# Unused matrix products placed ahead of the first stage of a convolution-attention kernel

## The chip, the cores and the metric

The kernel runs on one core of a Trainium2 chip. The metric is the device time of one execution in microseconds (us); lower is better. A core has five engines that run side by side, each working through its own instructions in order: TensorE (PE in the profile; its weight loads are listed as PEld), VectorE (DVE), ScalarE (ACT), GpSimd (POOL) and SyncE (SP), the last of which only issues transfers here.

## The reference, cut to what matters

The input `x` holds four images of 384 channels and 48 by 48 pixels. One attention layer with eight heads of 48 channels is computed, and its query gets a convolution added to it:

```python
local = conv_general_dilated(x, conv_w, (1, 1), 'SAME', feature_group_count=C)   # 7x7, depthwise
local = local * inv + (bn_beta - bn_mean * inv)
x_norm = layernorm(x_flat) * ln_gamma + ln_beta        # over the 384 channels of a token
q, k, v = x_norm @ qkv_w.T + qkv_b                     # split into 8 heads of 48
q = q + layernorm(local_flat)
out = softmax(q @ k.T * 48 ** -0.5) @ v                # 2304 tokens per image
out = x_flat + out @ proj_w.T + proj_b
```

## The kernel before, in words

Channels lie on the 128 partitions in three chunks. The four images are worked through in turn, each in five row tiles of 8 or 10 image rows (384 or 480 tokens). For one row tile the attention goes in twelve slots. In each slot TensorE multiplies queries and keys in products over 64 partitions (L1143; queries and keys are held as a rounded part and a rest, in the type that the program calls HALF, `float32r`, so three products make one score), ScalarE takes the exponential (L1151), and TensorE multiplies with the values in plain fp32 (L1158). In the profile a plain fp32 product appears as two matmul records with a weight load each, a `float32r` product as one.

VectorE computes the depthwise convolution of the next row tile in between, one tap at a time (L367). A list of time budgets, worked out when the program is built, sets how many taps are issued at which point of the TensorE program; so the order on every engine is fixed by the program text.

Ahead of the row tiles comes a first stage, for the keys, values and queries of image 0. Its order is written out by hand:

- SP loads the first image rows (`slab`), the weights (`staged`) and the rest of image 0 (`xn`) through one queue (L116). ACT's queue loads the small vectors.
- DVE builds `packing`, a set of 0/1 matrices that reorder channels (L222, L224), and `natural`, the taps with the batch norm folded in (L228 to L233).
- TensorE runs `warm(WARM)`, 14 products of two constant matrices whose result nobody reads (L1201). Then `pack()` multiplies `packing` by `natural` (L242), from which ACT copies `vec` (L249): the taps, shifts and gains that later steps use.
- `bias_rows()` makes two small tables on DVE (L276 to L280).
- The first 384 tokens are normalised in three blocks: means of `slab` (L729), centring on DVE (L644), squares on ACT (L583), means of those (L729), the root on ACT (L652 to L654) and on DVE (L666, L667), the scaling (L724). Meanwhile ACT scales the weights by the gains (L943, L950, L951).
- Then TensorE makes values, queries and keys group by group (L729 again, through `project`), and DVE's first convolution taps (L363, L367) and the later groups' norms run beside it.

PSUM tiles come from one pool of four double banks (`two_banks`), taken in turn. The SBUF tiles that matter here come from rotating buffers with a tag: `sq` has two, `acc` three.

The lines around the change are these:

```python
    def warm(n):
        m = two_banks()[:, 0, 0:P]
        for _ in range(n):
            nc.tensor.matmul(m, lhsT=mean_w, rhs=ident, start=True, stop=True)

    warm(WARM)
    pack()
    bias_rows()
```

Of the kernel before, what the change touches and what calls it, by code (L numbers as in the profile page):

```python
# [10 lines left out]
F32 = mybir.dt.float32  # L11
HALF = mybir.dt.float32r
# [4 lines left out]
P = 128  # L17
# [33 lines left out]
def unshifted_pass(  # L51
# [16 lines left out]
    nc = tc.nc  # L68
# [14 lines left out]
    GM = max(ROWS) * W  # L83
# [5 lines left out]
    def size(a):  # L89
        return a.stop - a.start  # L90
# [6 lines left out]
    work = ctx.enter_context(tc.tile_pool(name="work", bufs=2))  # L97
# [10 lines left out]
    def two_banks(name="r"):  # L108
        return ps.tile([P, 2, 512], F32, tag="r", name=name)
# [102 lines left out]
    for c in range(CC):  # L212
        for r, n, first in ((0, HD, 0), (64, HD, 1), (48, 16, 6), (112, 16, 7)):
            head = first + 2 * c if first < 6 else first
            ch = head * HD + (16 * c if first >= 6 else 0)
            while n:
                part = min(n, P - ch % P)
                pieces.append((c, r, ch // P, ch % P, part))
                r, n, ch = r + part, n - part, ch + part
# [17 lines left out]
    def pack():  # L237
        m = two_banks()[:, 0, 0 : CC * (T0 + 3)].rearrange("p (c v) -> p c v", c=CC)
        for c in range(CC):
            mine = [pair for pair in pairs if pair[0] == c]  # L240
            for pair in mine:
                nc.tensor.matmul(  # L242
                    m[:, c, :],
                    lhsT=packing[:, pairs.index(pair), :],
                    rhs=natural[:, pair[1], :],
                    start=pair == mine[0],
                    stop=pair == mine[-1],
                )
        nc.scalar.copy(vec, m)  # L249
# [23 lines left out]
    def bias_rows():  # L273

        rows = chosen_rows.rearrange("p a (j x) -> p a j x", j=2)
        nc.vector.memset(chosen_rows, 0.0)  # L276
        nc.vector.tensor_copy(
            rows[:, 0, :, 0:HD], ident[:, 0 : 2 * HD].rearrange("p (j d) -> p j d", j=2)
        )
        nc.vector.tensor_copy(  # L280
            rows[:, 1:4, :, HD:64],
            ident[:, 0 : 2 * HD].rearrange("p (j c r) -> p c j r", j=2, c=CC),
        )
# [610 lines left out]
    rows = {}  # L894
# [303 lines left out]
    def warm(n):  # L1198
        m = two_banks()[:, 0, 0:P]
        for _ in range(n):  # L1200
            nc.tensor.matmul(m, lhsT=mean_w, rhs=ident, start=True, stop=True)  # L1201

    warm(WARM)
    pack()
    bias_rows()

# [304 lines left out]
    for i, at in enumerate(pieces_out):  # L1511
        ao, n = aos[i], size(at)
        if i == 3:
            judge[1](two_banks()[:, 0, :])
        r, r2 = two_banks(), two_banks()
# [17 lines left out]
def conv_attention(tc: tile.TileContext, *args):  # L1533
    nc = tc.nc
    few = NH * max(ROWS) * 48 // P
    with tc.tile_pool(name="keep", bufs=1) as keep:
        inside = keep.tile([P, few], F32, tag="inside", name="inside")
        outside = keep.tile([P, few], F32, tag="outside", name="outside")
        ones = keep.tile([P, 1], F32, tag="ones_col", name="ones_col")
        total = keep.tile([1, 1], F32, tag="total", name="total")  # L1540
        flag = keep.tile([1, 1], mybir.dt.int32, tag="flag", name="flag")
        counts = []
        nc.vector.memset(inside, 1.0)
        nc.vector.memset(ones, 1.0)

        def compare():
            nc.vector.tensor_scalar(outside, inside, 0.5, None, ALU.is_lt)

        def count(m):
            counts.append(m[0:1, :few])  # L1550
            nc.tensor.matmul(counts[0], lhsT=ones, rhs=outside, start=True, stop=True)

        def decide():
            nc.vector.tensor_reduce(total, counts[0], AX.X, ALU.add)
            nc.vector.tensor_copy(flag, total)

        def read():
            return nc.values_load(flag[0:1, 0:1])

        n_outside = unshifted_pass(tc, *args, inside, (compare, count, decide, read))  # L1560
        with tc.If(n_outside > 0):
            shifted_pass(tc, *args)
# [505 lines left out]
```

## Time and profile before

| What | Value |
|---|---|
| Median of 3 runs | 2723.55 us (2722.94 to 2723.92) |
| Profiled execution | span 2720.3 us from its first to its last instruction; no time of its own is listed beside that, and the median of the runs lies 3.25 us above the span |
| TensorE busy | 2707.9 us, 100% of the span |
| VectorE busy | 2314.8 us, 85% |
| ScalarE busy | 1671.1 us, 61% |
| GpSimd busy | 592.7 us, 22% |
| Granted TensorE clock | 9 (90% or more) in each of the 40 slices of the page |

A row of a timeline gives the start and the length in us, the engine, the line and the operation, the tile written and the tile read, and the count of merged records; a bracket tells how long the engine stood idle just before and what ended that. TensorE's records are pipelined: one lasts from its start until its modelled end, and the next may start earlier, so the step from one record to the next is read from the starts. In the list of waits a row gives the total, the number and the longest of the waits. The chain of waits is followed back from the last instruction of the program.

### The profile page before, as it was taken

The numbers are of one execution on the slowest core, as the hardware profiler recorded it, in microseconds if no ns is written. First come the engines' busy times: TensorE is split into PE (matmuls) and PEld (weight loads), VectorE is DVE, ScalarE is ACT, GpSimd is POOL, SyncE is SP. The second block draws the span as 40 slices with busy tenths as digits, with TensorE's granted clock in tenths as the row PEclk, the third lists the DMA queues.
The fourth block names the chain that finished last, engine by engine and source line by source line (L and its number), as shares of the span: only waits on it lengthen the run. The fifth ranks groups of instructions, "written<-read, shape, count | busy, mean of one in ns | idle before, by whom it ended". The sixth has DMA issues, their size and how long they took to land.

```text
span 2720.3 us, 46072 instructions
## 1 busy us (share of the span) xinstructions
PE 2707.9 (100%) x16468; PEld 1532.5 (56%) x16468; DVE 2314.8 (85%) x4042; ACT 1671.1 (61%) x2318; POOL 592.7 (22%) x1061
## 2 busy tenths in 40 slices
PE   9999999999999999999999999999999999999999
PEld 6565555555566555555555655555555665555555
DVE  8999999989899999989889999889889898986212
ACT  4366767777326777777622767767752377676762
POOL 3541111112452111011165111111225501110110
PEclk9999999999999999999999999999999999999999
DMA  8454544545455545455455554544635544444442
GB/s 176 91 160 124 140 125 127 134 129 160 129 139 164 145 118 142 124 143 138 122 152 144 154 146 120 139 132 129 167 96 160 151 141 123 147 128 132 139 151 68
DMA packets 160129, 370.46 MB, mean 136 GB/s; under 512 B 58273, under 2 KB 107234, under 8 KB 159890
## 3 DMA queue, kind: packets, MB, share of 16 engines
q0 software_dynamic: 70688, 277.77, 36.0%
q1 hardware_dynamic: 83456, 79.29, 12.9%
q10 hardware_dynamic: 5746, 10.36, 1.1%
q8 instruction: 132, 2.16, 0.3%
q14 instruction: 107, 0.88, 0.1%
HBM read 258.14 MB, written 64.14 MB: 118 GB/s over the span
## 4 chain that ended last, share of the span: by engine, by line
PE 93%; DVE 5%; DMA 1%; ACT 0%; issue 0%; SPq 0%; DVEq 0%; ACTq 0%
PE o L1158 41%; PE r L1143 33%; PE r L729 18%; DVE acc L367 4%; DMA xn<-in_x_dram 1%; DMA staged<-in_qkv_wT_dram 0%; PE r L616 0%; DVE k L839 0%; DMA slab<-in_x_dram 0%; DVE sq L593 0%; DVE ao L1054 0%; SPq L116 0%; PE r L634 0%; DVE xn L644 0%; DVE sq L594 0%
## 5 line engine op out<-in xcount | busy, mean ns | idle before, releaser
L367 DVE SCALAR_TENSOR_TENSOR acc<-slab,vec,acc 128x470 f32<-128x470 f32 (+10 forms) x2832 | 1656.9, 656 | 2.0 <-ACT acc L330 2.0
L1151 ACT ACTIVATE pt<-r 128x960 f32<-128x960 f32 (+1 forms) x1440 | 1248.4, 943 | 244.1 <-PE o L1158 150.4
L1158 PE MATMUL o<-pt,v 128*64 128x480 f32 (+1 forms) x5760 | 1166.1, 554 | 0.4 <-ACT pt L1151 0.4
L1143 PE MATMUL r<-qs,ks 64*128 64x480 f32 (+1 forms) x8640 | 965.8, 373 | 1.6 <-ACT xn L853 0.7
L1143 PEld LDWEIGHTS r<-qs,ks 64*128 64x128 f32 x8640 | 783.6, 184 | 265.6 <-issue 168.2
L1158 PEld LDWEIGHTS o<-pt,v 128*64 128x64 f32 x5760 | 392.9, 137 | 659.2 <-issue 566.8
L801 POOL DMA_DIRECT2D ks<-wide x220 | 159.9, 727 | 1375.7 <-PE r L1143 1333.1
L729 PE MATMUL r<-xn,w_qk 128*128 128x384 f32 x864 | 284.2, 486 | 0.0
L1035 ACT COPY o<-o 113x480 f32<-113x480 f32 (+1 forms) x160 | 87.0, 544 | 275.6 <-PE o L1158 275.4
L729 PEld LDWEIGHTS r<-xn,w_qk 128*128 128x128 f32 x864 | 164.0, 190 | 114.7 <-issue 0.7
L823 ACT COPY v<-r 128x384 f32<-128x384 f32 x72 | 32.0, 480 | 190.3 <-PE r L729 190.3
L729 PE MATMUL r<-w_v,xn 128*128 128x384 f32 x432 | 145.0, 488 | 0.9 <-ACT sq L654 0.5
L1054 DVE TENSOR_TENSOR ao<-ao,o 113x480 f32<-113x480 f32 (+1 forms) x120 | 75.8, 631 | 75.2 <-ACT o L1035 75.2
L729 PEld LDWEIGHTS r<-w_v,xn 128*128 128x128 f32 x432 | 81.4, 190 | 59.9 <-issue 2.9
L786 POOL DMA_DIRECT2D wide<-k x144 | 71.7, 500 | 115.5 <-ACT k L836 79.4
L1011 DVE TENSOR_TENSOR qs<-xn,qs 128x480 fp32r<-128x480 f32 (+1 forms) x60 | 38.0, 633 | 59.1 <-ACT qs L1006 59.1
L729 PE MATMUL r<-af,w_o 128*128 128x384 f32 (+1 forms) x270 | 85.2, 470 | 0.0
L1045 ACT COPY ao<-o 113x480 f32<-113x480 f32 (+1 forms) x60 | 32.6, 544 | 74.3 <-PE o L1158 74.3
L1054 DVE TENSOR_TENSOR aot<-aot,o 113x480 f32<-113x480 f32 (+1 forms) x40 | 25.2, 631 | 58.5 <-ACT o L1035 58.5
L853 ACT ACTIVATE xn<-r,qkb 128x384 f32<-128x384 f32 x72 | 40.2, 577 | 55.1 <-PE r L729 53.8
L1124 DVE SCALAR_TENSOR_TENSOR xr<-r,pb,xr 128x384 f32<-128x384 f32 (+2 forms) x72 | 42.0, 611 | 36.8 <-PE r L729 28.1
L729 PEld LDWEIGHTS r<-af,w_o 128*128 128x128 f32 x270 | 51.3, 190 | 31.9
(154 smaller groups left out, 1338.8 us busy)
## 6 DMA issues: line engine op xcount, KB each, us to landing
ks<-wide POOLq DMA_DIRECT2D x220, 768.0 KB, 5.1
qs<-qs SPq DMA_DIRECT2D x346, 60.0 KB
slab<-in_x_dram POOLq DMA_DIRECT2D x22, 432.0 KB, 6.4
wide<-k POOLq DMA_DIRECT2D x96, 96.0 KB, 2.2
wide<-ks POOLq DMA_DIRECT2D x12, 768.0 KB, 5.1
xr<-in_x_dram POOLq DMA_DIRECT2D x16, 576.0 KB, 5.4
rb<-rden SPq DMA_DIRECT2D x32, 270.0 KB
held<-ao POOLq DMA_DIRECT2D x12, 720.0 KB, 4.1
```

What stands on the lines that cost most here:

```text
L367: nc.vector.scalar_tensor_tensor(dst, src, weight, dst, ALU.mult, ALU.add)
L729: nc.tensor.matmul(dst, lhsT=weights(c), rhs=src(c), start=c == 0, stop=c == CC - 1)
L786: nc.gpsimd.dma_start(out=last[16 * u : 16 * u + 16, 0], in_=k[r : r + 16, 0])
L801: queue.dma_start(out=place_keys(b, p, i), in_=wide[b, p][:, :, at])
L853: nc.scalar.activation(src[:, i, :], q[:, :G], AF.Identity, bias=qkb[:, 0, i : i + 1])
L1011: nc.vector.tensor_sub(qs[:, 1, :], query_of(t, p), qs[:, 0, :])
L1035: nc.scalar.copy(part[0 : 64 + HA], sums[0 : 64 + HA, 0, :n])
L1054: nc.vector.tensor_add(dst, dst, part[0 : 64 + HA])
L1124: nc.vector.scalar_tensor_tensor(xr[:, co, :], m, pb[:, co : co + 1], xr[:, co, :], ALU.add, ALU.add)
L1143: nc.tensor.matmul(r[:, j, :n], lhsT=ks[rows, w, at], rhs=qs[rows, m, :], start=i == 0, stop=i == 2,)
L1151: nc.scalar.activation(pt, r[:, :, :n], AF.Exp, scale=SCALE)
L1158: nc.tensor.matmul(sums[halves[j], 0, : columns_of(t)], lhsT=values[t // NA, kb // NB][:, first : first + 64], rhs=pt[:, j, :], start=i == ...
```

## The change

Between `warm` and `pack`, products are put in whose results nobody reads. Four DVE instructions prepare their operands: two fills of 128x480 with ones (`probe_in`, `probe_w`) and two copies of these into the type `float32r` (`probe_half`, `probe_w_half`). The helper `probe(rows, w, x, n, times)` takes a double bank and issues, `times` times, one product for each of the row tiles named, the j-th row tile into the j-th bank. All have 128 columns of weights. The lists `four` and the argument `spread` are not used.

| Call | Operands | Row tiles | Columns | Products |
|---|---|---|---|---|
| 1 | `float32r` | all 128 partitions | 480 | 5 |
| 2 | `float32r` | two of 64 | 480 | 10 |
| 3 | `float32r` | the first of 64 alone | 480 | 5 |
| 4 | fp32 | two of 64 | 480 | 4 |
| 5 | fp32 | all 128 partitions | 480 | 2 |
| 6 | `float32r` | all 128 partitions | 384 | 5 |

```diff
@@ -1200,7 +1200,32 @@
         for _ in range(n):
             nc.tensor.matmul(m, lhsT=mean_w, rhs=ident, start=True, stop=True)
 
+    probe_in = work.tile([P, GM], F32, tag="sq", name="probe_in")
+    probe_w = work.tile([P, GM], F32, tag="sq", name="probe_w")
+    for a in (probe_in, probe_w):
+        nc.vector.memset(a, 1.0)
+    probe_half = work.tile([P, GM], HALF, tag="acc", name="probe_half", bufs=3)
+    nc.vector.tensor_copy(probe_half, probe_in)
+    probe_w_half = work.tile([P, GM], HALF, tag="acc", name="probe_w_half", bufs=3)
+    nc.vector.tensor_copy(probe_w_half, probe_w)
+
+    def probe(rows, w, x, n, times, spread=False):
+        r = two_banks()
+        for i in range(times):
+            for j, a in enumerate(rows):
+                o = r[:, j, :n]
+                nc.tensor.matmul(o, lhsT=w[a, 0:P], rhs=x[a, :n], start=i == 0, stop=i == times - 1)
+
+    every = [slice(0, P)]
+    two = [slice(0, 64), slice(64, 128)]
+    four = [slice(32 * i, 32 * i + 32) for i in range(4)]
     warm(WARM)
+    probe(every, probe_w_half, probe_half, GM, 5)
+    probe(two, probe_w_half, probe_half, GM, 5)
+    probe(two[:1], probe_w_half, probe_half, GM, 5)
+    probe(two, probe_w, probe_in, GM, 2)
+    probe(every, probe_w, probe_in, GM, 2)
+    probe(every, probe_w_half, probe_half, 384, 5)
     pack()
     bias_rows()
 
```

On TensorE, at the start of the program of the changed kernel (the rows are instructions; before, L242 followed directly on L1201):

```order
L1201 MATMUL r<-ident,mean_w 128x128 x14
L1217 MATMUL r<-probe_half,probe_w_half 128x480 x20
L1217 MATMUL r<-probe_in,probe_w 128x480 x6
L1217 MATMUL r<-probe_half,probe_w_half 128x384 x5
L242 MATMUL r<-natural,start_up 128x52 x7
L729 MATMUL r<-slab_0_115,mean_w 128x128 x9
```

All 31 products stand ahead of `pack` and of the means of the first block.

On VectorE, between the end of `natural` and the tables of `bias_rows` in the changed kernel:

```order
L233 TENSOR_SCALAR natural<-start_up,inv 128x49 x3
L1206 MEMSET probe_in 128x480
L1206 MEMSET probe_w 128x480
L1208 CAST probe_half<-probe_in 128x480
L1210 CAST probe_w_half<-probe_w 128x480
L276 MEMSET spread 128x512
L277 COPY spread<-ident 128x2x48
```

The four new instructions stand behind `natural`, although the program text calls for nothing of it there; before, L276 followed directly on L233.

## The prediction, made before the run

> **What bounds the kernel now.** I read the page first: busy times, then the chain of waits.
>
> ```profile
> PE 2707.9 (100%) x16468; PEld 1532.5 (56%) x16468; DVE 2314.8 (85%) x4042; ACT 1671.1 (61%) x2318; POOL 592.7 (22%) x1061
> PE 93%; DVE 5%; DMA 1%; ACT 0%; issue 0%; SPq 0%; DVEq 0%; ACTq 0%
> ```
>
> TensorE is idle for 2720.3 - 2707.9 = 12.4 us in all, and 93% of the chain runs on it. So the next view is the list of what TensorE waited for over the whole span:
>
> ```profile
> PE r L1201 <- POOL one L169: 1.8, 1, 1.8
> PE r L616 <- ACT sq L588: 1.0, 1, 1.0
> PE r L634 <- DVE sq L594: 0.7, 2, 0.4
> PE r L1143 <- ACT xn L853: 0.7, 1, 0.7
> PE r L729 <- ACT sq L654: 0.5, 1, 0.5
> PE r L1143 <- DMA qs<-qs: 0.5, 1, 0.5
> PE r L729 <- DVE xn L724: 0.4, 2, 0.2
> PE r L1143 <- ACT pt L1151: 0.4, 1, 0.4
> PE o L1158 <- ACT pt L1151: 0.4, 1, 0.4
> ```
>
> After its first instruction TensorE waits for 4.6 us in 2700, mostly for engines that it feeds itself. A busy TensorE need not be at its peak, so I looked at the start in the timeline of TensorE, whose rows follow each other without a hole from the warm-up to the values:
>
> ```profile
> 1.81 4.76 PE L1201 MATMUL r<-ident,mean_w 128*128 128x128 f32 x28 [1.81 <-POOL one L169]
> 6.41 1.66 PE L242 MATMUL r<-natural,start_up 128*128 128x52 f32 x14
> 7.91 2.24 PE L729 MATMUL r<-slab,mean_w 128*128 128x128 f32 x18
> 10.01 1.61 PE L729 MATMUL r<-sq,mean_w 128*128 128x128 f32 x12
> ...
> 13.68 4.11 PE L729 MATMUL r<-w_v,xn 128*128 128x384 f32 x12 [0.50 <-ACT sq L654]
> ```
>
> The warm-up ends where `pack` begins, at 6.41. What TensorE does next feeds everything: ACT takes `vec` from `pack`, DVE centres with the means of 7.91, ACT squares what DVE centred. What is put in ahead of `pack` therefore delays the three engines together, and a TensorE that is never long idle later cannot make it up.
>
> **The change part by part.** It removes and moves nothing. It adds four instructions on DVE and 31 products on TensorE.
>
> *DVE.* The four stand behind `natural`. The timeline of DVE there, before:
>
> ```profile
> 5.86 0.55 DVE L233 TENSOR_SCALAR natural<-start_up,inv 128x49 f32<-128x49 f32 x3
> 6.46 0.48 DVE L276 MEMSET spread<- 128x512 f32 x1
> 6.98 0.21 DVE L277 COPY spread<-ident 128x96 f32<-128x96 f32 x1
> 7.11 0.24 DVE L280 COPY spread<-ident 128x96 f32<-128x96 f32 x1
> 8.84 1.89 DVE L644 TENSOR_TENSOR xn<-slab,r 128x384 f32<-128x384 f32 x3 [1.49 <-PE r L729]
> ```
>
> The first fill can start at 6.46. Durations come from the groups of DVE by shape, and for the type `float32r` from the page:
>
> ```profile
> L224 DVE COPY start_up<-ident 128x16 f32<-128x16 f32 x8 | 1.1, 175 | 0.0
> L222 DVE MEMSET start_up<- 128x896 f32 x1 | 0.8, 805 | 0.2 <-issue 0.2
> L224 DVE COPY start_up<-ident 128x48 f32<-128x48 f32 x4 | 0.7, 189 | 0.1
> L1011 DVE TENSOR_TENSOR qs<-xn,qs 128x480 fp32r<-128x480 f32 (+1 forms) x60 | 38.0, 633 | 59.1 <-ACT qs L1006 59.1
> ```
>
> A fill costs 0.83 ns a column (805 ns for 896 against 485 for L276's 512; the 0.48 above), so 0.46 for 480: two take 0.92. No copy of 480 columns is in the trace. From below: the copies of 16 and 48 columns rise by 0.44 ns a column, which gives 0.38 us; from above, L1011, which also writes 480 `float32r` columns but reads two operands, 0.63. I take 0.45, nearer to the copies because one operand is read. So the operands are ready at 6.46 + 0.92 + 0.04 (the step from a fill to a dependent copy, 6.46 to 6.98 less 0.48) + 0.90 = 8.32 (8.18 to 8.68), and the first product starts at about 8.4. The DVE time itself costs nothing more: `bias_rows` then ends about two us later than 7.35, while DVE's next work, L644, waits for TensorE until far beyond that. If that cover were gone it would cost 1.9 us. TensorE, however, is done with the warm-up at 6.57 and now stands idle for some 1.8 us, because the products wait for the copies.
>
> *TensorE.* Three pairs of rows price the products: the score and value products of a slot with 480 columns, the score products with 384, and the projections at the end with 480 columns and all partitions.
>
> ```profile
> 1110.36 5.05 PE L1158 MATMUL o<-pt,v 128*64 128x480 f32 x24
> 1115.34 4.17 PE L1143 MATMUL r<-qs,ks 64*128 64x480 f32 x36
> 1119.44 5.05 PE L1158 MATMUL o<-pt,v 128*64 128x480 f32 x24
> ...
> 160.11 3.43 PE L1143 MATMUL r<-qs,ks 64*128 64x384 f32 x36
> 163.47 4.09 PE L1158 MATMUL o<-pt,v 128*64 128x384 f32 x24
> ...
> 2706.97 7.41 PE L729 MATMUL r<-ao,w_o 128*128 128x480 f32 x18
> 2708.18 0.19 PEld L729 LDWEIGHTS r<-ao,w_o 128*128 128x128 f32 x1 [0.21 <-issue]
> 2708.58 0.19 PEld L729 LDWEIGHTS r<-ao,w_o 128*128 128x128 f32 x1 [0.21 <-issue]
> ```
>
> - Call 2, ten `float32r` products in two row tiles: exactly the form of L1143. From 1115.34 to 1119.44 are 4.10 us for 36, 0.114 each: 1.14.
> - Calls 1 and 3, five each of all partitions or of one row tile alone, are not in the trace. If two row tiles at a time run beside each other, one pass takes twice 0.114, 0.228; that is the value I take, 1.14 for each call. Bounds: 0.114 (no running beside each other at all, the row tile alone no dearer), and 0.806, the full-array fp32 product (weight loads follow at 0.40, two to a product), if `float32r` had no shorter way over the full array. The nearest row is L1143, the same type.
> - Call 6, 384 columns: 3.36 us for 36, so 0.187 for a pass, five are 0.93.
> - Call 5, two fp32 products over all partitions: 2 x 0.806 = 1.61.
> - Call 4, four fp32 products in two row tiles. From below half the full-array price, as L1158 shows for two column tiles (4.98 us for 12, 0.415 each): 1.66. From above no overlap, 4 x 0.806 = 3.22. I take 1.66; L1158 has the type and the halves, if on the other side of the array.
> - Changes between row-tiled and full-array products, two of them: the L1158 block of 12 lasts 4.98 against 12 x 0.403 = 4.84, so 0.14 at most for entering it; I add 0.2 for both.
>
> Sum: 1.14 + 1.14 + 1.14 + 1.66 + 1.61 + 0.93 + 0.20 = 7.8 us, so `pack` starts at 8.4 + 7.8 = 16.2 in place of 6.41. By then `natural` is long there. Everything that hangs on `pack` and on the first means is late by 9.8.
>
> *What could take some of it back.* The loads do not move, so a wait for a load would shrink. TensorE has none in the first stage; its one wait for a transfer, 0.5 for `qs`, is for a copy of queries that are late too. I take 0.1 back, with 0.5 as the bound. Row tiles and slots after that follow each other on TensorE as before. The span becomes 2720.3 + 9.7 = 2730.0; with the 3.25 us by which the median of the runs exceeds the span, 2733.3 us, 0.36% more.
>
> *The clock.* Two stretches of the warm-up show how TensorE speeds up:
>
> ```profile
> 1.81 1.44 PE L1201 MATMUL r<-ident,mean_w 128*128 128x128 f32 x5 [1.81 <-POOL one L169]
> ...
> 4.11 2.46 PE L1201 MATMUL r<-ident,mean_w 128*128 128x128 f32 x18
> ```
>
> Of 28 records the first ten take 2.30 us (1.81 to 4.11), the other 18 take 2.30 until `pack`: 0.23 against 0.128 a record. If the new hole of 1.8 us undid that, the first 2.3 us of the products would do what 1.3 us do at speed: 1.0 us more, inside the range. The Trainium skill ("TensorE: Matmul & The Clock Gate", Part 1) says that the gate closes only after an idle window of about 3.4 us, by which this hole costs nothing; no run here shows a hole of that length.
>
> **The rivals.**
>
> *Weights that can't be loaded ahead (slower still).* In the row tiles of L1143 each next product lies in the other half of the array, so its weights can be loaded beside the running one. In calls 1, 3 and 6 each product uses the rows of the one before. If the load then stands in line, 15 products pay up to 0.19 (the weight loads above) more: 2.9 us, and the time is 2736.2. Against it: in the projections at the end each load of 0.19 falls within the 0.40 step of its record, over the same 128 rows. That is fp32, not `float32r`, and a step is twice as long, so it isn't settled. The same skill page (Part 3, what overlaps and what doesn't) states that a weight load overlaps a running matmul only where the row group differs; by that rule the 2736.2 would come out. The rows at 2708 disagree with it for fp32.
>
> *Dearer products (slower still).* If `float32r` over the full array needs as long as fp32, calls 1 and 6 cost 5 x (0.806 - 0.228) + 5 x (0.645 - 0.187) = 5.2 more (0.645 is 0.806 x 384/480); if call 4 does not overlap, 1.6. That is 2735 to 2740.
>
> *The loads hide it (not slower).* The chain of waits runs, from its start until 38.15, through loads and their issue, not engines:
>
> ```profile
> 33.85 4.27 DMA xn<-in_x_dram
> 38.12 0.03 issue
> 38.15 1.14 DVE k L839 x2
> 39.29 0.48 DVE sq L593
> ```
>
> If the load that lands at 38.12 set the first stage, a start of the engines 9.8 us late would vanish in front of it, and the time would stay at about 2723.6. It decides if an engine stands idle for that load. Against it, from the timeline of DVE:
>
> ```profile
> 36.88 1.36 DVE L724 SCALAR_TENSOR_TENSOR xn<-xn,sq 128x1152 f32<-128x1152 f32 x1
> 38.15 1.14 DVE L839 SCALAR_TENSOR_TENSOR k<-r,qkb,k 128x384 fp32r<-128x384 f32 x2
> 39.20 0.55 DVE L593 TENSOR_TENSOR sq<-xn 128x384 f32<-128x384 f32 x1
> ```
>
> No bracket stands behind any of them: DVE goes from work to work, and the sums of the loaded group come more than a microsecond after the landing. The load is just in time, not late; it can give nothing back.
>
> *The later waits absorb a part.* If the 4.6 us of waits after the first instruction shrank to nothing, the gain would be at most that: 2728.7. But nine of the ten waits are for ACT or DVE work that TensorE's own late results start.
>
> **How the numbers follow.** The forecast, 2731.5 to 2735: 70%. Weights or dearer products, 2735 to 2740: 20%. Absorbed in part, 2728.5 to 2731.5: 5%. Hidden by loads: 4%. Faster by something not seen: 1%. The range runs from 2730.0 to 2737.0. A measurement of this kernel tells about 0.2% from no change, 5.4 us; to stay below it the products would have to take less than 3.5 us (the operands alone bring two), and even at the lower bounds, 0.114 for each of the 20 long `float32r` products and 0.093 for each of the five short ones, they take 2.28 + 0.47 + 1.66 + 1.61 = 6.0. So slower by over 0.2%: 94%; within: 5%; faster: 1%.
>
> **What would show it.** In the changed profile: the four DVE rows between 6.46 and about 8.3; a hole on TensorE with the copy as its end, some 1.8 us long; L1217 from about 8.4 to 16.2, with the steps priced above; L242 at about 16.2; DVE's L644 at about 18.6 (8.84 + 9.8); TensorE's total idle time some 2 us higher and the later waits as before. I am wrong if L242 comes before 12 or after 20, or if it comes at 16 and the span has grown by less than 8: then something later did absorb it.

## The result, and the profile after

| | Before | Changed |
|---|---|---|
| Median of 5 runs | 2723.55 us (2722.94 to 2724.64) | 2732.72 us (2731.72 to 2733.49) |
| Span of the profiled execution | 2720.3 us | 2730.1 us |
| Ratio of the times | | 1.0033, 95% interval 1.0022 to 1.0045 |

The forecast was 2733.3 us for the runs and 2730.0 for the span. The page's first line and the list of what TensorE waited for, of the changed kernel:

```profile
PE 2716.4 (99%) x16505; PEld 1537.7 (56%) x16505; DVE 2317.0 (85%) x4046; ACT 1671.7 (61%) x2318; POOL 594.7 (22%) x1061
PE r L1217 <- DVE probe_w_half L1210: 1.2, 1, 1.2
PE r L616 <- ACT sq L588: 0.9, 1, 0.9
PE r L729 <- DVE xn L724: 0.8, 3, 0.4
```

TensorE is busy for 8.5 us more and idle for 1.3 us more (13.7 against 12.4). The one new line among the waits is the hole of 1.2 us in front of the products; the others are those of before within 0.4 us. So nearly all of the 9.8 us of span are the products and the hole. The start of TensorE in the timeline:

```profile
1.81 4.76 PE L1201 MATMUL r<-ident,mean_w 128*128 128x128 f32 x28 [1.81 <-POOL one L169]
7.80 3.51 PE L1217 MATMUL r<-probe_half,probe_w_half 128*128 128x480 f32 x19 [1.22 <-DVE probe_w_half L1210]
...
15.66 1.66 PE L242 MATMUL r<-natural,start_up 128*128 128x52 f32 x14
17.15 2.24 PE L729 MATMUL r<-slab,mean_w 128*128 128x128 f32 x18
```

`pack` (L242) starts at 15.66 in place of 6.41, 9.25 late; the means of the first block at 17.15 in place of 7.91, 9.24 late. From there the order is that of before, shifted. Three rows further on, before (the first and the last are from the chain of waits, the middle one is from the timeline of TensorE):

```profile
122.91 13.53 PE r L729 x54
...
802.42 5.97 PE L729 MATMUL r<-w_v,xn 128*128 128x384 f32 x18
...
1351.41 139.52 PE r L729 x432
```

And the same three in the changed kernel:

```profile
132.18 13.53 PE r L729 x54
...
812.30 3.17 PE L729 MATMUL r<-w_v,xn 128*128 128x384 f32 x9 [0.43 <-DVE xn L724]
...
1361.42 139.52 PE r L729 x432
```

The delay is 9.27 us at the first row and still 9.28 just ahead of 802 us. There TensorE waits for the scaling on DVE (L724), where it had no wait before, and the delay grows to 9.98; from then on it stays at 10.0. So 9.25 us of delay pass through, and 0.7 us come in at this one place; the span, at 9.8 us more, loses 0.2 of it behind these rows. This wait does not follow the size of the delay: in runs shown below, the one with the products doubled, 18 us late by then, gains nothing there, and the one with products only further on, 0.9 late by then, gains 0.4. What decides it was not tested.

On DVE, before and behind the products:

```profile
7.08 0.35 DVE L1208 CAST probe_half<-probe_in 128x480 fp32r<-128x480 f32 x1
7.34 0.40 DVE L1210 CAST probe_w_half<-probe_w 128x480 fp32r<-128x480 f32 x1
...
8.44 0.25 DVE L280 COPY spread<-ident 128x96 f32<-128x96 f32 x1
18.09 1.90 DVE L644 TENSOR_TENSOR xn<-slab,r 128x384 f32<-128x384 f32 x3 [9.40 <-PE r L729]
```

`bias_rows` is done at 8.69 and DVE then waits 9.40 us for the means: its four new instructions lie in a hole, and its own work starts 9.25 late with everything else.

### The profile page after: what moved, and what is told of

Its sections match the earlier page's. It is cut to its first block, busy times and chain, and to the rows that moved or that the text cites. A ratio compares the mean times of both kernels' runs of the same rounds, so it can differ in the third digit from the quotient of the medians.

```text
span 2730.1 us, 46150 instructions
## 1 busy us (share of the span) xinstructions
PE 2716.4 (99%) x16505; PEld 1537.7 (56%) x16505; DVE 2317.0 (85%) x4046; ACT 1671.7 (61%) x2318; POOL 594.7 (22%) x1061
## 4 chain that ended last, share of the span: by engine, by line
PE 90%; DVE 7%; DMA 2%; issue 0%; ACT 0%; SPq 0%; POOL 0%; DVEq 0%; POOLq 0%; ACTq 0%
PE o L1158 41%; PE r L1143 33%; PE r L729 16%; DVE acc L367 5%; DMA slab<-in_x_dram 0%; DMA wide<-k 0%; DVE k L839 0%; DMA staged<-in_qkv_wT_dram 0%; PE r L616 0%; DMA xn<-in_x_dram 0%; DVE xn L724 0%; DVE sq L594 0%; SPq L116 0%; DVE sq L593 0%; DVE xr L1124 0%
## 5 line engine op out<-in xcount | busy, mean ns | idle before, releaser
L1143 PE MATMUL r<-qs,ks 64*128 64x480 f32 (+1 forms) x8640 | 965.9, 373 | 1.6 <-ACT xn L853 0.7
L1143 PEld LDWEIGHTS r<-qs,ks 64*128 64x128 f32 x8640 | 783.6, 184 | 265.6 <-issue 168.2
```

Of the source, the lines that this page charges most:

```text
L1143: nc.tensor.matmul(r[:, j, :n], lhsT=ks[rows, w, at], rhs=qs[rows, m, :], start=i == 0, stop=i == 2,)
```

## The experiments

The theory: what holds up TensorE ahead of `pack` arrives at the end one for one. The rivals: a part comes through DVE, or loads or later waits absorb a part.

### Only the four DVE instructions

```diff
     warm(WARM)
-    probe(every, probe_w_half, probe_half, GM, 5)
...
-    probe(every, probe_w_half, probe_half, 384, 5)
     pack()
```

> The four DVE instructions of the change are kept, all 31 products are left out. Theory (only what holds up TensorE ahead of pack counts): the DVE work is hidden while DVE waits for the first means; bias_rows ends at about 9.0 instead of 7.35 and the first centring (L644) may start 0.1 to 0.3 late, pack still starts at about 6.4; 2723.6 us, as before. Rival (DVE's own lateness is part of the 9.2 us): L644 1.6 late, 2725.2 us.

Measured: 2723.19 us against 2723.30 before, ratio 0.9999 (0.9990 to 1.0009). TensorE and DVE in its timeline:

```profile
1.81 5.53 PE L1201 MATMUL r<-ident,mean_w 128*128 128x128 f32 x28 [1.81 <-POOL one L169]
7.17 1.66 PE L242 MATMUL r<-natural,start_up 128*128 128x52 f32 x14
...
8.66 0.24 DVE L280 COPY spread<-ident 128x96 f32<-128x96 f32 x1
9.61 1.89 DVE L644 TENSOR_TENSOR xn<-slab,r 128x384 f32<-128x384 f32 x3 [0.70 <-PE r L729]
```

DVE still waits for TensorE at L644, so none of the 9.2 us came through DVE. The cover is nearly used up, though: `bias_rows` ended at 8.90, and in the profile before, L644 started at 8.84. That `pack` started at 7.17 and not at 6.41 has nothing to do with DVE (no bracket stands behind L242); it is the warm-up, which took 5.53 us here against 4.76. More on that at the end.

### The operands made early

```diff
+    probe_in = work.tile([P, GM], F32, tag="sq", name="probe_in")
...
+    nc.vector.tensor_copy(probe_w_half, probe_w)
     nc.vector.memset(packing, 0.0)
```

> The change with its four DVE instructions put ahead of packing, so that the operands are ready before the warm-up ends. Theory: the hole of 1.2 us between warm-up and first product goes, the products start at about 6.5, pack at about 14.4 instead of 15.66, and the time is 1.2 us below the changed kernel: 2731.5 us. Rival (the hole is covered by something else that is late, such as a load): pack earlier but the end unmoved, 2732.7 us.

Measured: 2731.13 us (2730.47 to 2731.93), ratio to before 1.0029 (1.0018 to 1.0040). TensorE there (the insertion moves `pack` from L242 to L250):

```profile
1.81 5.30 PE L1209 MATMUL r<-ident,mean_w 128*128 128x128 f32 x28 [1.81 <-POOL one L169]
6.86 3.48 PE L1217 MATMUL r<-probe_half,probe_w_half 128*128 128x480 f32 x19
...
14.68 1.66 PE L250 MATMUL r<-natural,start_up 128*128 128x52 f32 x14
```

The hole is gone, and `pack` starts 0.98 earlier than in the changed kernel. In the chain of waits the row that stood at 132.18 there is 1.00 earlier too:

```profile
131.18 13.53 PE r L737 x54
```

The hole was on the path, and up to 802 us what it cost comes through one for one. The runs alone do not show that: the medians lie 7.8 us (here) and 9.2 us (the change) above those measured beside them, and the intervals of the two ratios overlap. The spans, 2728.6 against 2730.1, are of one execution each, and part of their difference is the wait of 802 us, which adds 0.3 here and 0.7 in the changed kernel.

### The products twice

```diff
     probe(every, probe_w_half, probe_half, 384, 5)
+    probe(every, probe_w_half, probe_half, GM, 5)
...
+    probe(every, probe_w_half, probe_half, 384, 5)
     pack()
```

> The change with its six calls issued twice. Theory (what is put ahead of pack arrives at the end one for one): pack 7.7 later than in the changed kernel (7.80 to 15.66, less the warm-up of the row tiles), at about 23.4, and 2740.4 us. Rival (loads or later waits absorb part of a delay, or more of it once it is larger): pack at the same 23.4, but the end below 2738 us.

Measured: 2739.25 us, ratio 1.0058 (1.0043 to 1.0074), that is 15.95 us above before.

```profile
1.81 5.83 PE L1201 MATMUL r<-ident,mean_w 128*128 128x128 f32 x28 [1.81 <-POOL one L169]
8.04 3.51 PE L1217 MATMUL r<-probe_half,probe_w_half 128*128 128x480 f32 x19 [0.41 <-DVE probe_w_half L1210]
...
23.63 1.66 PE L242 MATMUL r<-natural,start_up 128*128 128x52 f32 x14
```

`pack` is 7.97 later than in the changed kernel. In the chain of waits the row of 132.18 is 7.95 later:

```profile
140.13 17.49 PE r L729 x66
```

That is 17.22 us behind the row of before (122.91), as `pack` is: a delay of 17 us passes as one of 9 does. The median is 1.2 us below the expected 2740.4, within the interval (11.7 to 20.2 us above before), and above the 2738 of the rival.

The span of this execution, the slowest of the four, is 8.2 us longer than that of the changed kernel (2738.3 against 2730.1), but that is no second proof: 0.7 of the shorter one is the wait of 802 us, and 1.05 of this one has another cause. The first score products of the row tiles take longer here:

```profile
168.67 0.41 PE L1143 MATMUL r<-qs,ks 64*128 64x384 f32 x1 [0.73 <-ACT xn L853]
169.49 5.39 PE L1143 MATMUL r<-qs,ks 64*128 64x384 f32 x35 [0.41 <-DMA qs<-qs]
...
170.80:174.10 3.30, 3.30 (x24) 3.30 (x22) 3.30 (x7) 3.00 (x4) 3.30 (x7) 0.50 0.65 145
```

Before, with holes of 0.72 and 0.48 us at the same place, they took 3.83 us:

```profile
152.33 3.83 PE L1143 MATMUL r<-qs,ks 64*128 64x384 f32 x35 [0.48 <-DMA qs<-qs]
```

The row of 170.80:174.10 gives the busy times in that stretch, in the order PE, PEld, DVE, ACT, POOL; the figure behind POOL's is the granted clock, here 0.50. The delay grows to 18.9 us there, a wait for ACT at 247 us (L616) takes 0.65 back, and 18.27 are left. Why the clock fell in this execution is open.

### Products in the middle of the row tiles

```diff
         for s in range(NSLOT):
+            if t == 8 and s == 6:
+                r = two_banks()
+                for i in range(10):
+                    nc.tensor.matmul(r[:, 0, :C], lhsT=mean_w, rhs=w_v[:, 0, :], start=i == 0, stop=i == 9)
             score_batch(t, s)
```

> The kernel before, with ten unread fp32 products over all partitions, 384 columns, in the middle of the row tiles (row tile 8, slot 6) and nothing at the start. Their price by the projections of the trace is 10 x 0.645 = 6.45 us. Theory (TensorE is the bound throughout, so its time is worth the same wherever it lies): 2730.0 us. Rival (the start is special, since everything hangs on it there, while in the row tiles waits of TensorE or the spare time of the others absorb an insertion): below 2727 us.

Measured: 2729.37 us against 2722.99, 6.38 more (6.45 expected); ratio 1.0023 (1.0013 to 1.0033). Their line in the trace (shortest, median and longest duration in ns, then the first and last start in us):

```profile
L1407 PE MATMUL r<-w_v,mean_w x20: 486/486/590, 1189.3 to 1195.5; 128*128 128x384 f32 x20
```

The start is not special: in the timeline the delay against before is 1.32 us ahead of these products and 7.96 behind them, 6.64 more, and it stays so to the end. This is the strongest evidence that TensorE bounds the kernel beyond its start, though it is one place of many.

### The means ahead of `pack`

If a delay passes through, does a gain? The means of the first block need only their load.

```diff
-WARM = 14
+WARM = 8
...
-    pack()
-    bias_rows()
...
-    for at in blocks:
+    for i, at in enumerate(blocks):
         norm.mean_of(raw, at)
+        if i == 2:
+            pack()
         norm.centre(raw, at)
         norm.squares(at)
+    bias_rows()
```

> The kernel before, without the products: the means of the first block go ahead of pack, bias_rows goes behind the centring, and the warm-up is cut from 14 to 8 products, so that TensorE's first useful product starts when its load has landed (about 4.9) instead of at 6.41. Theory (the start passes to the end one for one, in this direction too): the first values start at about 11.6 to 12.2 instead of 13.68, the time falls by 1.5 to 2.0 us to about 2721.8 us. Rival (the loads are just in time, so a gain ends where one binds): the load of the third group, which landed at 38.1 with 1.1 us to spare, holds DVE up at L593, a wait for a load appears there, and the gain is at most 1.1 us: 2722.5 us.

Measured: 2722.79 us against 2723.30, ratio 1.0002 (0.9993 to 1.0011): no change that can be told. The eleven runs fall into groups, six from 2722.11 to 2722.79, four from 2724.23 to 2724.79 and one at 2727.20; the profile is of the first group, and what lengthens the others is not known. Neither expectation was right:

```profile
1.81 3.78 PE L1201 MATMUL r<-ident,mean_w 128*128 128x128 f32 x16 [1.81 <-POOL one L169]
7.12 2.25 PE L729 MATMUL r<-slab,mean_w 128*128 128x128 f32 x18 [1.53 <-DMA slab<-in_x_dram]
9.20 1.66 PE L242 MATMUL r<-natural,start_up 128*128 128x52 f32 x14
...
14.22 4.11 PE L729 MATMUL r<-w_v,xn 128*128 128x384 f32 x12 [0.39 <-ACT sq L654]
```

TensorE waits until 7.12 for the first image rows. I had read their landing from the chain of waits before, where a piece of the load's queue ends at 4.8; the image rows come in four transfers, and TensorE had to wait for the last until 2.3 us later. So the means move from 7.91 to 7.12 only, `pack` then stands in their way, and the first values start at 14.22 instead of 13.68. A load does limit the first stage after all, but another one than the rival had named, and if it lands alike under the order of before, it has 0.8 us to spare there (7.12 against 7.91). It limits what an earlier start can gain; it does not absorb a later one. At the third group no wait for a load appeared, so the 1.1 us there remain untested.

### Holes of several lengths

The hole of 1.22 us cost its length and no speed. How long may it be? DVE fills ahead of the last step of `natural` hold `pack` up:

```diff
+    fill = work.tile([P, GM], F32, tag="sq", name="fill")
+    fill_b = work.tile([P, GM], F32, tag="sq", name="fill_b")
+    for i in range(10):
+        nc.vector.memset((fill, fill_b)[i % 2], 1.0)
     for c in range(CC):
         nc.vector.tensor_scalar(
```

> The kernel before, with ten fills on DVE ahead of the last step of natural, so that TensorE stands idle for about 4.5 us between warm-up and pack. Theory (the delay of pack arrives at the end, and the hole costs no speed): pack at about 11.0, 4.6 late, 2728.2 us. Rival (a hole of this length undoes the speed-up that the warm-up brought): pack and the first means then run at 0.23 us a record instead of 0.11 for the next 2.3 us, about 1 us more, 2729.2 us; the steps of L242 and L729 in the trace tell it. The rule of about 3.4 us in the Trainium skill (TensorE: Matmul & The Clock Gate, Part 1) is on the rival's side here.

> The same with five fills: a hole of about 2.2 us. Theory: pack at about 8.7, 2.3 late, records of L242 at 0.107 us a step as before; about 2725.9 us. Rival (any hole slows TensorE down): steps of 0.2 us and more at L242. The rule of the Trainium skill (3.4 us) is on the theory's side here.

Measured with ten fills: 2730.50 us against 2722.99, ratio 1.0027 (1.0017 to 1.0036). With five, a single run: 2724.20. TensorE with ten fills, and the busy times of the engines in three stretches (the insertion moves `pack` to L246 and the means to L733):

```profile
10.89 3.23 PE L246 MATMUL r<-natural,start_up 128*128 128x52 f32 x14 [3.79 <-DVE natural L237]
13.91 4.17 PE L733 MATMUL r<-slab,mean_w 128*128 128x128 f32 x18
```

```profile
7.20:9.20 2.00, 0.00 (x0) 0.00 (x0) 1.80 (x5) 0.00 (x0) 0.00 (x0) 1.00 0.96 181
9.30:10.80 1.50, 0.00 (x0) 0.00 (x0) 1.38 (x5) 0.00 (x0) 0.00 (x0) 0.50 1.13 180
10.90:19.40 8.50, 8.50 (x40) 8.50 (x41) 2.75 (x8) 1.86 (x4) 0.00 (x0) 0.50 1.12 184
```

The rival held in this execution, and at a higher price than it named: the clock falls to 0.50 within the hole, and after the hole it stays there for 8.5 us. `pack` starts 4.48 later than before, the first values (21.99 against 13.68) 8.31 later: 3.8 us of speed lost beside 4.5 us of delay. The ten runs lie between 2728.20 and 2731.25; the lowest is what the theory had expected, so the clock may not fall in every execution. With five fills the hole came out at 1.35 us, since the warm-up ended later than I had reckoned, and the clock stayed:

```profile
8.27 1.84 PE L246 MATMUL r<-natural,start_up 128*128 128x52 f32 x14 [1.35 <-DVE natural L237]
```

Nine and seven fills lie in between.

> Nine fills in place of ten: pack at about 10.3, a hole of 3.2 to 3.8 us (the end of the warm-up moves between executions from 6.4 to 7.5). If the granted clock falls to 0.50 as with ten, pack's 14 records take 3.0 us and the time is about 2730.0 us; if a hole of this length is still free, 1.5 us and about 2726.5 us. By the rule of about 3.4 us (the Trainium skill, TensorE: Matmul & The Clock Gate, Part 1) it may go either way.

> Seven fills: pack at about 9.3, a hole of 2.0 to 2.8 us. Theory (a hole below the 3.79 us of the ten fills costs only its own length): pack's 14 records in 1.5 us, about 2725.5 us. Rival (2 us are already enough to lose the speed): 3.0 us for pack, granted clock 0.50, about 2729 us.

Measured, a single run each: 2729.30 with nine, 2728.59 with seven (before 2722.09 beside them). Seven fills:

```profile
9.54 3.23 PE L246 MATMUL r<-natural,start_up 128*128 128x52 f32 x14 [2.59 <-DVE natural L237]
...
7.00:8.90 1.90, 0.00 (x0) 0.00 (x0) 1.75 (x4) 0.00 (x0) 0.00 (x0) 1.00 0.97 198
8.95:9.50 0.55, 0.00 (x0) 0.00 (x0) 0.52 (x3) 0.00 (x0) 0.00 (x0) 0.50 1.10 162
```

In a hole of 2.59 us the clock was halved; so it was in that of nine fills:

```profile
10.36 3.23 PE L246 MATMUL r<-natural,start_up 128*128 128x52 f32 x14 [3.02 <-DVE natural L237]
```

The holes at the start that left the clock alone were 1.22, 1.35 and 1.53 (the wait for the load in the run with the means first). A fall costs some 3 us here: with seven fills from L246 to the first values 10.3 us pass (9.54 to 19.86), before 7.3 (6.41 to 13.68).

The length of the hole is not all that counts. By the traces' records of the clock it rose at 5.51, 6.32 and 5.83 us (seven, nine, ten fills) and fell at 8.92, 9.73 and 9.24, each time 3.41 us after the rise and 2.0 to 2.4 us into the hole. It then stayed low for 6.83, 6.83 and 10.24 us, twice, twice and three times that step. So in these runs the clock changed in steps of 3.41 us, and where a hole lies between two of them probably counts as well, though no run varied that alone. The run with the doubled calls lost the clock after holes of only 0.73 and 0.41 us. At the start no hole between 1.53 and 2.59 us was measured.

### fp32 products in two row tiles

```diff
-    probe(every, probe_w_half, probe_half, GM, 5)
...
-    probe(every, probe_w_half, probe_half, 384, 5)
+    probe(two, probe_w, probe_in, GM, 8)
+    probe(every, probe_w, probe_in, GM, 8)
```

> The change with only its fp32 products: eight pairs in two row tiles, then eight products over all partitions. In the changed kernel the two pairs took 2.1 us (10.95 to 13.07) where 1.66 was expected. Theory (two row tiles run beside each other at full value, and the first and last half of a group run alone): steps of 0.40 us to two records, eight pairs 0.81 each and 0.5 to 0.6 once, about 7.0 us; the eight full products 6.45. Rival (fp32 row tiles overlap only in part): 1.06 a pair, 8.5 us.

A single run (2737.44 us; 14.5 above before):

```profile
7.53 0.67 PE L1217 MATMUL r<-probe_in,probe_w 64*128 64x480 f32 x2
...
14.17 6.71 PE L1217 MATMUL r<-probe_in,probe_w 128*128 128x480 f32 x16
...
20.71 0.54 PE L242 MATMUL r<-natural,start_up 128*128 128x52 f32 x4
```

Eight pairs from 7.53 to 14.17 are 0.83 each, eight products over all partitions from 14.17 to 20.71 are 0.82 each. Two row tiles of fp32 run fully beside each other, and a pair costs what one full product costs. The 7.0 expected for the pairs was 0.4 too much: the halves that I thought ran alone at both ends do not show as extra time.

## Why the prediction was right

**The bound.** "A TensorE that is never long idle later cannot make it up": shown by the ten products in the middle (6.38 measured, 6.45 priced) and by the doubled calls, whose 17.22 us of delay are still 17.22 at 140 us, not only by the shift of the rows of the change.

**The sum.** That the span came out within 0.1 of the forecast (2730.1 against 2730.0) is luck. `pack` started at 15.66 and not at 16.2, 0.5 us less delay than reckoned; the wait of 0.7 at 802 us, which the prediction did not have, made up for it.

**DVE.** Forecast: operands ready at 8.32 (8.18 to 8.68), a hole of 1.8 us. Measured: 7.74 and 1.22. Two terms were off. `natural` was done 0.26 earlier in this execution (the first fill began at 6.20, not 6.46); that is scatter between executions, for in the run with DVE alone it began at 6.42. And the copies took 0.35 and 0.40, with 0.26 from one start to the next, below my 0.45 each and for one of them below my lower bound of 0.38. The choice between the bounds went half way to a row with two operands; the copies' own slope was the better guide. "Costs nothing more" was right, with less to spare than I had said: `bias_rows` ended some 1.5 us later, at 8.90, where L644 had started at 8.84.

**TensorE.** By calls, from start to start: 1.29, 1.20, 1.08 and 1.70 for the first four (1.14, 1.14, 1.14 and 1.66 priced), 2.59 for the fifth and sixth (2.54 priced). Sum 7.86 against 7.8 with the 0.2 for changes between forms. Call 1 takes 0.33 to its second record and 0.31 from its last to the next call, in place of 0.22; most of that 0.2 went there. Call 4 is counted here from the end of call 3; its first product starts at 10.95, beside the last products of call 3, and counted from there call 4 takes the 2.1 us that the expectation of the last experiment names.

**Weights that can't be loaded ahead.** This rival (2736.2) fell with the rows of calls 1 and 3; here narrow stretches of the timeline, each beginning with the start of a record:

```profile
8.12 0.59 PE L1217 MATMUL r<-probe_half,probe_w_half 128*128 128x480 f32 x2
8.34 0.59 PE L1217 MATMUL r<-probe_half,probe_w_half 128*128 128x480 f32 x2
...
10.29 0.59 PE L1217 MATMUL r<-probe_half,probe_w_half 64*128 64x480 f32 x2
10.51 0.59 PE L1217 MATMUL r<-probe_half,probe_w_half 64*128 64x480 f32 x2
```

The step is 0.22 over the full array and 0.22 in one row tile alone, the price of a pair of L1143 (0.228), although each load of weights (0.18 to 0.19 us) goes to the rows that the running product uses. So a load is hidden in the rows of its own predecessor, in `float32r` as in fp32. That is against the rule of the Trainium skill ("TensorE: Matmul & The Clock Gate", Part 3) that I had set against it; the same Part also lets a load go ahead into a background buffer for weights, and that these rows do not contradict. They also settle "dearer products" for `float32r`: one row tile alone, two together and the whole array all take 0.22 for 480 columns. For fp32 in row tiles the last experiment does, with 0.83 a pair.

**Loads hide it.** No load took anything back: with 17 us of delay at `pack` the rows at 140 us are 17.22 late, with 9.25 they are 9.27 late at 132. The first group's load does set how early the stage can start, which I had not seen.

**The clock.** That the hole costs no speed held at 1.22 us, but the reason that I leaned on did not. I had given a relapse a price of 1.0 us, and the hole that the forecast itself foresaw, 1.8, lies in the stretch where nothing was measured. A hole of 2.59 us cost 3 us beside its length. Had the operands come 1.4 us later, the forecast could have been some 3 us short (an estimate from the run with seven fills). The Trainium skill's window of about 3.4 us (the same page, Part 1) would have called that hole harmless; the step of 3.41 us stands in the traces, but TensorE was idle for only 2.0 to 2.4 us of it when the clock fell, and the measurement decides. The 0.128 us a record that the prediction took for the full speed is mixed, too: its stretch began at 4.11, while the steps change from 0.21 to 0.11 at 4.71.

**Span and median.** 3.25 us lay between the span of before and the median of its runs. For single executions the two differ by less: the profiled one of the changed kernel took 2731.97 us with a span of 2730.1, 1.87 more. So the profiled execution of before was one of the faster ones, and its `pack` at 6.41 was early, against 7.17 in the run with DVE alone. That fits a span that grew by 9.8 and a median that grew by 9.2. The 3.25 in the forecast was too much, and with 1.87 it would have been 2731.87 us, 0.85 below the median that was measured.

## What to carry to other kernels

Where the list of waits leaves the busiest engine almost no idle time, work put on it costs its own duration (at both places tried here), and work on another engine costs nothing while that engine waits. Price a product from rows of the same type and row use, and reckon with the holes around it: at the start, holes on TensorE of up to 1.5 us cost their length, and one of 2.6 us cost twice that. Read the granted clock behind a hole before you rely on either. Before moving work ahead, look for the last transfer that it needs, not for a piece of the chain.

## What I had not expected of the hardware

The moment at which TensorE speeds up is not fixed. The same 14 warm-up products took 4.76 us in the profiles of before and of the change, and 5.53, 5.30 and 5.83 in those shown above; another:

```profile
1.81 5.79 PE L1201 MATMUL r<-ident,mean_w 128*128 128x128 f32 x28 [1.81 <-POOL one L169]
```

This is from the run with fp32 products alone. The steps of their records are 0.21 us at first and 0.11 later, and in narrow stretches of the timeline the change comes at 4.7 us in the first two and at 6.9 in this one, though all begin at 1.81. When it comes late, `pack` waits for the warm-up instead of `natural`: 7.17 against 6.41. In the changed kernel the hole swallows this. That it makes up part of the scatter of the runs before, 2722.1 to 2724.6 us, is argued, not shown.

The granted clock reads 1.00 in the stretch from 2 to 4 us, where these steps are twice as long, and 0.50 after a long hole, where they are as long again. The first record of the clock in the trace of before begins at 4.71, with the change of the steps. At the start of a program the steps of the records tell the speed, not that column.

In the hole of 3.79 us the low clock lasted 10.2 us, 8.6 of them with products running, longer than the 3 to 5 us from the first product to the change at the start of the program.
